# RWKV attention with a Hadamard feed-forward layer: the first two products of two tiles as one split into seven

## Chip, cores and metric

The kernel runs on one core of a Trainium2 chip. The metric is the time of one execution in device microseconds (us); it was measured three times.

## What is computed

All arrays are fp32. x is 4 x 2048 x 512, and xn is x normalized over its last axis (layer norm without weights). The result is x plus an attention part and a feed-forward part, both of xn:

```python
shifted = jnp.pad(xn, ((0, 0), (1, 0), (0, 0)))[:, :-1]
xr, xk, xv = (mu * xn + (1.0 - mu) * shifted for mu in (mu_r, mu_k, mu_v))
r, k, v = xr @ Wr.T, xk @ Wk.T, xv @ Wv.T            # 512 x 512 weights
# the recurrence over t, by batch and channel, with w_eff = -exp(w)
p   = maximum(pp, u + k_t);    e1  = exp(pp - p);           e2  = exp(u + k_t - p)
y_t = (e1 * aa + e2 * v_t) / (e1 * bb + e2)
p2  = maximum(w_eff + pp, k_t); e1b = exp(w_eff + pp - p2);  e2b = exp(k_t - p2)
aa, bb, pp = e1b * aa + e2b * v_t, e1b * bb + e2b, p2
attention = (sigmoid(r) * y) @ Wo.T
hidden = silu(xn @ W1.T) * (xn @ W3.T)               # W1, W3: 2048 x 512
feed_forward = fwht(hidden) @ W2.T                   # Walsh-Hadamard, 1/sqrt(2048)
```

## The kernel before

**Blocks and stages.** Channels lie on the partitions, tokens along the free axis. The 8192 tokens are worked on in 8 blocks of 1024 (`TB`), two blocks for a batch. A block has three stages: r, k and v (six chunks of weights), the gate and the linear part (16 tiles `j`, of 128 hidden channels each), and the down stage, which multiplies by W2 and Wo; the Hadamard transform is folded into W2 in block 0. Block 0 also makes sums of the weights on GpSimd and keeps them in DRAM (`part_w`), from which later blocks load.

**Seven products.** Matrix products are done in Strassen's manner in Winograd's form: a 2 x 2 split of weights and rows needs seven products where the plain way needs eight. A chunk of weights, loaded into a ring of three buffers (`ring_a`, by `load_parts`), holds seven forms: form 0 is the block 11 itself, form 4 the first of the sums, and so on. Channels (512) and tokens (1024) are halved; for a tile of the gate and linear part, gate (W1) and linear (W3) rows are the two halves of the weights. Each product then has 256 channels, two matmuls of 128, on 512 columns (`H`). `seven` takes five of the eight PSUM banks in turn, runs the products in the order of forms 0, 4, 5, 1, 3, 6, 2, and lets partial results move from bank to bank: ScalarE copies `pa` to `pb` after form 0, `pf` to the SBUF tile `s5` after form 4, `pb` to `pc` after form 5 and `pb` to `pd` after form 3; VectorE adds `s5` to `pb` and `pc`. `up` finishes a tile: silu(gate) * linear by tanh on ScalarE and products on VectorE, the last four of them (`tail`) in the middle of the next tile.

**The recurrence.** `wkv(h)` is written for one head of 128 channels as a generator that stops nine times. Its scans run on VectorE over 1024 tokens. A call of `step()` runs the next piece; `up` calls it twice a tile, after `h0` and after the sum on `pc`, and nine pieces of the first head are run beside r, k and v by `hook` in blocks 1 to 7. The exponents are differences from a running maximum that VectorE subtracts: `b1`, `e1b`, `e1` and `k` are each made by an instruction of their own and then go through Exp on ScalarE.

**Order.** Every engine keeps the order in which the source issues its instructions (`InOrder`, line 35 in the profile, is the line of all of them). An instruction waits on semaphores where it needs another engine's result or space, and whatever stands behind it on its engine waits with it. SyncE issues the DMAs, in the same manner.

**The down stage** already uses a second level: `Deep` splits a product on 11 once more into seven of 256 columns (`lo`, `hi`), with the banks `a`, `b` and `f`, and `s5` for `f`'s copy. `pieces_w` holds its weights, eight pieces in turn.

Of the kernel before, what the change touches and what calls it, by code (L numbers as in the profile page):

```python
# [2 lines left out]

# [37 lines left out]
def tile_rwkv_attn_hadamard_ffn(  # L41
# [36 lines left out]

    down_w = dram.tile([2, 7, KH, P, QR, P], F32, name="down_w")
    deep_w = dram.tile([6, 7, P, QR, P], F32, name="deep_w")  # L80
    stat_d = dram.tile([n_blocks, 2, TB], F32, name="stat_d")


# [6 lines left out]
    sa, sb = (const.tile([P, OFF + TB], F32, name=n) for n in ("sa", "sb"))  # L90
    e1b, e1 = (const.tile([P, TB], F32, name=n) for n in ("e1b", "e1"))
    banks = [ps.tile([P, H], F32, name=f"bank{b}") for b in range(8)]
    turn = [0]

    NP = NF // 2

# [16 lines left out]
        return flat[:, 0:size].rearrange(f"p ({' '.join(names)}) -> p {' '.join(names)}", **dict(zip(names, shape)))  # L113

    def bank():
        turn[0] += 1
        return banks[(turn[0] - 1) % 8]


    k_flat, v_flat = (t.rearrange("p b t -> p (b t)") for t in (k_sb, v_sb))  # L120
    tf_flat = tf.rearrange("p f k t -> p (f k t)")
    x_first, x_tok = (flat.rearrange("p (t c) -> p t c", c=C) for flat in (k_flat, tf_flat))
    spread = v_sb[:, 0:2, :]
    stage = [v_sb[:, 2 + s // 2, ts(s % 2, H)] for s in range(4)]
    u2_of = [e1b[:, ts(g, H)] for g in range(KH)]
# [142 lines left out]
    def wkv(h):  # L268
        w_h, u_h = weff[:, h : h + 1], vec[:, 4, h : h + 1]
        r, k, v = (row_of(kind, h) for kind in range(3))  # L270
        a0, a1, b0, b1 = sa[:, OFF - 1 : OFF - 1 + TB], sa[:, OFF : OFF + TB], sb[:, OFF - 1 : OFF - 1 + TB], sb[:, OFF : OFF + TB]
        first_a, first_b, last_a, last_b = a0[:, 0:1], b0[:, 0:1], a1[:, TB - 1 : TB], b1[:, TB - 1 : TB]
        tt, stt, scan, copy = dve.tensor_tensor, dve.scalar_tensor_tensor, dve.tensor_tensor_scan, dve.tensor_copy
        cy = [carry[:, h, n : n + 1] for n in range(3)]

        def exp(t):
            act.activation(t, t, AF.Exp)


        copy(first_a, cy[0])  # L280
        scan(a1, w_h.to_broadcast([P, TB]), k, first_a, ALU.add, ALU.max)
        tt(b1, k, a1, ALU.subtract)
        yield
        stt(e1b, a0, w_h, a1, ALU.add, ALU.subtract)
        stt(e1, k, u_h, a0, ALU.add, ALU.max)
        stt(k, k, u_h, e1, ALU.add, ALU.subtract)
        tt(e1, a0, e1, ALU.subtract)
        copy(cy[0], last_a)
        yield
        exp(b1)  # L290
        exp(e1b)
        yield

        copy(first_a, cy[1])
        tt(a1, b1, v, ALU.mult)
        scan(a1, e1b, a1, first_a, ALU.mult, ALU.add)
        copy(cy[1], last_a)
        yield
        exp(k)
        exp(e1)  # L300
        yield
        copy(first_b, cy[2])
        scan(b1, e1b, b1, first_b, ALU.mult, ALU.add)
        copy(cy[2], last_b)
        tt(v, k, v, ALU.mult)
        yield
        num, den = e1, e1b
        tt(den, e1, b0, ALU.mult)
        tt(den, den, k, ALU.add)
        dve.reciprocal(den[:, 0:H], den[:, 0:H])  # L310
        yield
        dve.reciprocal(den[:, H:TB], den[:, H:TB])
        yield
        tt(num, e1, a0, ALU.mult)
        tt(num, num, v, ALU.add)
        stt(r, r, 1.0, num, ALU.add, ALU.mult)
        stt(r, r, 0.5, den, ALU.mult, ALU.mult)
        yield
# [72 lines left out]
    def forms_in(t):  # L391
        seven_forms([t[:, n] for n in range(3, 7)], *(t[:, n] for n in range(4)))

    def load_parts(i, n):
        t = ring_a.tile([P, 7, KH, P], F32, tag="a", name=f"part_{i}_{n}")
        if is_first(i, n):
            sp.dma_start(out=t[:, 0:4], in_=wpart[n])
            forms_in(t)
        else:
            sp.dma_start(out=t, in_=part_w[n])  # L400
        return t

    def is_first(i, n):
        return i == (1 if n < 3 * KH else 0)
# [35 lines left out]
    def up(i, j, w, tail, step):  # L440

        keep_parts(i, 3 * KH + j, w)
        h0, h1 = unit(j)[:, 0:H], unit(j)[:, H:TB]

        def on11(pa):
            act.activation(h0, pa, AF.Tanh, scale=0.5)

        def on22(pa, pb, s5):
            dve.scalar_tensor_tensor(h0, h0, 1.0, pa, ALU.add, ALU.mult)
            step()  # L450
            dve.tensor_tensor(pb, pb, s5, ALU.add)

        def on12(pc, s5):
            dve.tensor_tensor(pc, pc, s5, ALU.add)
            step()

        pb, pc, pd = seven(f"{i}_{j}", w, right_of["up"], tail, on11, on22, on12)
        return (
            lambda: act.activation(h1, pc, AF.Tanh, scale=0.5),
            lambda: dve.tensor_tensor(h0, h0, pd, ALU.mult),  # L460
            lambda: dve.scalar_tensor_tensor(h1, h1, 1.0, pc, ALU.add, ALU.mult),
            lambda: dve.tensor_tensor(h1, h1, pb, ALU.mult),
        )

# [93 lines left out]
        program += deep(m, *which)  # L560
    DEEP_AT = (0, 4, 5, 6, 1, 3, 2)

    def piece(i, u):

        return pieces_w[:, (u + 4 - len(program if i else whole_program)) % 8]

    def load_piece(i, u):
        pieces = program if i else whole_program
        if u < len(pieces):
            kind, form, n = pieces[u]  # L570
            src = down_w[n[0], form, n[1]] if kind == "plain" else deep_w[form, DEEP_AT[n]]
            sp.dma_start(out=piece(i, u), in_=src)

    whole, lo, hi = slice(0, H), slice(0, H // 2), slice(H // 2, H)
    x11, x12, x22 = stage[0:2], stage[2:4], x22_of
# [19 lines left out]
    class Down:  # L595
# [21 lines left out]
            self.matmuls(pt, self.u - 1, rows, cols, start)  # L617

        def matmuls(self, pt, u, rows, cols, start=False):
            w = piece(self.i, u)  # L620
            for n in range(QR):
                pe.matmul(
                    pt[:, cols], lhsT=w[:, n, :], rhs=rows[:, n, :], start=start and n == 0, stop=n == QR - 1,
                    skip_group_check=True,
                )
# [299 lines left out]
    diag_1 = first_diagonals(1, first_statistics(1))  # L925

    def order_of(i):
        rkv, (first, *rest) = range(3 * KH), range(3 * KH, 3 * KH + NF)
        return [first, *rest] if i == 0 else [first, *rkv, *rest]

    class Chores:

# [26 lines left out]
    for i in range(n_blocks):  # L959
# [8 lines left out]
        def step():  # L968
            next(pieces, None)

        def group(n):

            order = order_of(i)
            if n + 2 < len(order):
                parts.append(load_parts(i, order[n + 2]))
            return parts.pop(0)


# [1 line left out]
        if i == 0:  # L980
            for kind, after in ((1, 2), (2, 0), (0, None)):
# [8 lines left out]
                for n in range(2 * NB):  # L990
# [11 lines left out]
                    if kind == 2 and n == 2:  # L1002
                        fold_evict(fold_products(5, NP))
                        folded = fold_butterflies()
            parts = [load_parts(i, n) for n in order_of(i)[:2]]
        else:


# [10 lines left out]
            for b in range(NB):  # L1019
                mix_here(1, b)  # L1020
            k_forms = mix_forms(1)
            tail = up(i, 0, group(0), tail, lambda: next(k_forms))
            for _ in k_forms:
                pass
            chores, hooks = mix_chores(2, 0), [0]
            for n in range(3 * KH):

                def hook():
                    hooks[0] += 1
                    for _ in range(1 if hooks[0] % 3 else 2):  # L1030
                        next(chores, None)
                    if hooks[0] in (5, 6, 8, 11, 12, 13, 14, 15, 17):
                        step()

                tail = projected_pair(i, n, group(1 + n), tail, hook)


        for j in range(0 if i == 0 else 1, NF):
            w = group(j if i == 0 else 3 * KH + j)
            if i == 0 and j <= NR:  # L1040
                if j > 1:
                    keep_down()
# [20 lines left out]
        def next_parts():  # L1063
            if not last:
                parts.extend(load_parts(i + 1, n) for n in order_of(i + 1)[:2])

        if not last:
            load_tokens(i + 1)
# [57 lines left out]
```

## Time and profile before

| | us |
|---|---|
| median of three runs | 3047.5 (3046.84 to 3048.74) |
| the profiled execution | 3048.46 |
| its span, first to last instruction | 3046.7 |
| TensorE busy | 3027.2 (99%) |
| VectorE busy | 2468.0 (81%) |
| ScalarE busy | 1014.6 (33%) |
| GpSimd busy | 231.9 (8%) |

In the profile PE is TensorE's matmuls, PEld its weight loads, DVE VectorE, ACT ScalarE, POOL GpSimd and SP SyncE. A row of a group gives line, engine, operation, output<-inputs, shape and count, then the busy time in us, the mean of one in ns, and the idle time of the engine just before them with what ended it. One matmul shows as two MATMUL records and two LDWEIGHTS. A row of the timeline gives start and duration in us, then the operation and how many follow each other. A matmul's modelled end lies beyond the start of the next, so the time that one costs is read from start to start. The cost of an instruction on VectorE and ScalarE is read likewise where the next did not wait.

### The profile page before, as it was taken

The page shows a single profiled execution, that of the slowest core. Times are in us where ns is not written, and L with a number is a line of the kernel's source. Part 1 is how long each engine was busy: PE and PEld are TensorE (multiplying, and loading weights), DVE is VectorE, ACT ScalarE, POOL GpSimd, SP SyncE. Part 2 cuts the span into 40 slices and gives each one's busy share as a digit, 9 for nine tenths or more (in the row PEclk, how much of TensorE's full clock was granted, in tenths as well). Part 3 has the DMA queues.
Part 4 walks back from the last instruction along what each step waited for, and adds up shares of the span by engine and source line. Part 5 has one row for each costly group of instructions (what it writes and reads, how often), then busy time and mean ns, then how long its engine had stood idle before and what let it go on. Part 6 is the DMA issues. An engine that isn't in the chain of part 4 may idle for free.

```text
span 3046.7 us, 24404 instructions
## 1 busy us (share of the span) xinstructions
PE 3027.2 (99%) x8492; PEld 1613.7 (53%) x8492; DVE 2468.0 (81%) x2579; ACT 1014.6 (33%) x1822; POOL 231.9 (8%) x192
## 2 busy tenths in 40 slices
PE   8999999999999999999999999999999999999999
PEld 3444444447644476444854448544484445844458
DVE  6798658897888888888887978789798887988876
ACT  4233224333243323433233332433324333243321
POOL 3363003220000000000000000000000000000000
PEclk9999999999999999999999999999999999999999
DMA  4264524666422264222632236322453224522234
GB/s 174 74 204 170 189 82 136 215 215 216 137 75 82 79 233 132 73 77 101 224 120 80 73 133 201 110 80 78 161 166 117 73 81 165 184 93 78 73 123 143
DMA packets 136058, 397.64 MB, mean 131 GB/s; under 512 B 14336, under 2 KB 32768, under 8 KB 133760
## 3 DMA queue, kind: packets, MB, share of 16 engines
q1 hardware_dynamic: 135936, 396.09, 37.8%
q8 instruction: 68, 1.11, 0.1%
q14 instruction: 54, 0.44, 0.0%
HBM read 336.08 MB, written 59.96 MB: 130 GB/s over the span
## 4 chain that ended last, share of the span: by engine, by line
PE 95%; DVE 3%; DMA 1%; POOL 1%; ACT 0%; issue 0%; SPq 0%; POOLq 0%; ACTq 0%; DVEq 0%
PE bank L35 95%; DMA pieces_w<-deep_w 1%; DVE right L35 1%; DVE e1b L35 1%; POOL rs L35 1%; DVE e L35 0%; DVE xnT L35 0%; DMA stat_d<-rs 0%; DVE sb L35 0%; DVE sa L35 0%; DVE bank L35 0%; DVE v_sb L35 0%; DMA right<-w 0%; SPq L35 0%; ACT tf L35 0%
## 5 line engine op out<-in xcount | busy, mean ns | idle before, releaser
L35 PE MATMUL bank<-tf,part 128*128 128x512 f32 x2048 | 941.7, 592 | 0.0
L35 ACT COPY bank<-bank 128x512 f32<-128x512 f32 (+1 forms) x638 | 337.1, 528 | 1414.2 <-PE bank L35 1383.7
L35 PE MATMUL bank<-right,pieces_w 128*128 128x256 f32 (+1 forms) x2928 | 791.5, 430 | 3.1 <-DVE v_sb L35 2.5
L35 PE MATMUL bank<-xnT,part 128*128 128x512 f32 x1536 | 722.1, 592 | 1.1 <-DVE right L35 1.1
L35 PEld LDWEIGHTS bank<-right,pieces_w 128*128 128x128 f32 x2928 | 557.0, 190 | 230.9 <-issue 166.9
L35 PEld LDWEIGHTS bank<-tf,part 128*128 128x128 f32 x2048 | 389.0, 190 | 490.1 <-issue 461.8
L35 PEld LDWEIGHTS bank<-xnT,part 128*128 128x128 f32 x1536 | 291.6, 190 | 366.9 <-issue 358.2
L35 DVE TENSOR_TENSOR right<-right 128x1280 f32<-128x1280 f32 (+2 forms) x236 | 327.8, 1415 | 64.7 <-PE bank L35 63.7
L35 PE MATMUL bank<-right,part 128*128 128x512 f32 x840 | 369.6, 593 | 0.0
L35 DVE SCALAR_TENSOR_TENSOR right<-right,bank 128x512 f32<-128x512 f32 x256 | 174.4, 681 | 220.5 <-ACT right L35 220.3
L35 PEld LDWEIGHTS bank<-right,part 128*128 128x128 f32 x840 | 158.4, 190 | 203.2 <-issue 189.4
L35 ACT ACTIVATE right<-bank 128x512 f32<-128x512 f32 x308 | 183.8, 600 | 124.1 <-PE bank L35 105.7
L35 DVE RECIPROCAL e1b<-e1b 128x512 f32<-128x512 f32 x64 | 214.1, 3347 | 1.1
L35 DVE TENSOR_TENSOR bank<-bank,s 128x512 f32<-128x512 f32 x256 | 168.7, 690 | 37.4 <-ACT bank L35 23.8
L35 DVE TENSOR_TENSOR right<-right,bank 128x512 f32<-128x512 f32 x256 | 173.5, 678 | 11.5 <-PE bank L35 7.1
L35 POOL TENSOR_SCALAR mean<-sums 128x8 f32<-128x8 f32 x7 | 5.8, 835 | 1870.3 <-ACT tf L35 1518.6
L35 DVE SCALAR_TENSOR_TENSOR right<-xnT,vec,right 128x1024 f32<-128x1024 f32 x92 | 119.6, 1336 | 14.3 <-ACT right L35 14.3
L35 ACT COPY s<-bank 128x512 f32<-128x512 f32 x128 | 75.0, 586 | 144.9 <-PE bank L35 144.8
L35 POOL TENSOR_TENSOR part<-part 128x256 f32<-128x256 f32 x88 | 89.4, 1027 | 200.9 <-DMA part<-wpart 99.3
L35 ACT ACTIVATE right<-xnT,omm 128x1024 f32<-128x1024 f32 x92 | 100.3, 1143 | 12.3 <-PE bank L35 12.3
L35 PE MATMUL bank<-pieces_w,part 128*128 128x512 f32 x224 | 100.7, 592 | 0.0
L35 PE MATMUL bank<-k_sb,pieces_w 128*128 128x256 f32 x420 | 97.5, 379 | 0.0
(120 smaller groups left out, 2297.9 us busy)
## 6 DMA issues: line engine op xcount, KB each, us to landing
part<-part_w SPq DMA_DIRECT2D x148, 896.0 KB, 4.6
pieces_w<-deep_w SPq DMA_DIRECT2D x294, 320.0 KB, 3.2
pieces_w<-down_w SPq DMA_DIRECT2D x80, 320.0 KB, 5.4
part_w<-part SPq DMA_DIRECT2D x22, 896.0 KB, 6.0
tf<-x SPq DMA_DIRECT2D x7, 2048.0 KB, 7.8
xnT<-xT SPq DMA_DIRECT2D x7, 2048.0 KB, 10.0
deep_w<-pieces_w SPq DMA_DIRECT2D x6, 2240.0 KB, 10.3
v_sb<-xT SPq DMA_DIRECT2D x48, 256.0 KB, 8.0
```

The lines of the kernel that those rows point to most:

```text
L35: return self.tc.keep_in_program_order(issue(*args, **kwargs))
```

## The change

From block 2 on the tiles 2 to 15 are worked on in seven pairs. For a pair, the products of form 0 (on 11) and of form 4 (the first sum) of both tiles are taken together, as one product with 256 rows of weights and 256 channels, and each of the two is split into seven products of one matmul on 256 columns. That makes 14 matmuls of 256 columns where there were 8 of 512. The five other products of each tile stay (`up_rest`).

- `make_pair` and `keep_pair` make the 14 forms of a pair in block 0 on GpSimd and write them to DRAM (`pair_w`); a pair's forms are one load of the ring, and a tile's five other forms (`rest`) another one, in two DMAs.
- `make_pair_sums` makes four sums of 256 columns for each of the two right sides, once a block, on VectorE, in `pieces_w`.
- `Pair.step` runs the seven products with numbers n = 0 to 6, in halves `lo` and `hi` of two banks, with copies on ScalarE between the halves, and sums on VectorE (`evict`).
- `up_pairs` weaves the 14 products of a pair between the products of the tile before it.
- Banks are taken from a list of free ones and given back (`take`, `give`).
- In the recurrence one difference stands for two exponents: `e1b` and `e1` are made by one instruction each, and Relu with scale 1 or -1 on ScalarE, then Exp with scale -1, makes the two from it. Three VectorE instructions of 1024 go for each head of each block, and four on ScalarE come.
- The place of a piece of `pieces_w` no longer depends on the program's length (`piece`).

```diff
         def exp(t):
-            act.activation(t, t, AF.Exp)
+            act.activation(t, t, AF.Exp, scale=-1.0)
+        def over(out, d, sign):
+            act.activation(out, d, AF.Relu, scale=sign)
         copy(first_a, cy[0])
         scan(a1, w_h.to_broadcast([P, TB]), k, first_a, ALU.add, ALU.max)
-        tt(b1, k, a1, ALU.subtract)
-        yield
-        stt(e1b, a0, w_h, a1, ALU.add, ALU.subtract)
-        stt(e1, k, u_h, a0, ALU.add, ALU.max)
-        stt(k, k, u_h, e1, ALU.add, ALU.subtract)
-        tt(e1, a0, e1, ALU.subtract)
+        stt(e1b, a0, w_h, k, ALU.add, ALU.subtract)
+        yield
+        stt(e1, k, u_h, a0, ALU.add, ALU.subtract)
         copy(cy[0], last_a)
+        over(b1, e1b, 1.0)
+        over(e1b, e1b, -1.0)
         yield
         exp(b1)
         exp(e1b)
...
         copy(cy[1], last_a)
+        over(k, e1, -1.0)
+        over(e1, e1, 1.0)
         yield
         exp(k)
         exp(e1)
...
+    def up_rest(which, tail, step):
+        j, lhs, pa, pb, s5 = which
...
+        yield
+        product(pb, 5, f2)
+        pc = take()
+        act.copy(pc, pb)
+        for f in tail:
+            f()
+        yield
+        product(pa, 1, m21)
+        act.activation(h0, pa, AF.Tanh, scale=0.5)
+        yield
+        product(pb, 3, f3)
+        dve.scalar_tensor_tensor(h0, h0, 1.0, pa, ALU.add, ALU.mult)
+        give(pa)
+        pd = take()
+        act.copy(pd, pb)
+        step()
+        dve.tensor_tensor(pb, pb, s5(), ALU.add)
+        yield
+        product(pc, 6, m22)
+        dve.tensor_tensor(pc, pc, s5(), ALU.add)
+        step()
+        yield
+        product(pd, 2, f4)
+        yield
+        return (
+            lambda: act.activation(h1, pc, AF.Tanh, scale=0.5),
+            lambda: dve.tensor_tensor(h0, h0, pd, ALU.mult),
+            lambda: dve.scalar_tensor_tensor(h1, h1, 1.0, pc, ALU.add, ALU.mult),
+            lambda: dve.tensor_tensor(h1, h1, pb, ALU.mult),
+            lambda: give(pd, pc, pb),
+        )
...
+        def step(self, d, *which):
+            q11, _, q21, q22 = pair_quarters(d)
+            t1, t2, t3, t4 = (pair_sums[:, d, n] for n in range(4))
+            for n in which:
+                if n == 1:
+                    self.banks[d] = [take(), take()]
+                a, b = self.banks[d]
+                pt, right = (
+                    (a[:, lo], q11), (a[:, hi], t1), (b[:, hi], t2), (a[:, hi], q22), (a[:, lo], q21), (b[:, hi], t3), (b[:, lo], t4),
+                )[n]
+                form = 7 * d + DEEP_AT[n]
+                pe.matmul(pt, lhsT=self.w[:, form], rhs=right, start=n == 1, stop=True, skip_group_check=True)
+                if n == 0:
+                    act.copy(b[:, hi], a[:, lo])
+                elif n == 1:
+                    act.copy(pair_s5[:, d], a[:, hi])
+                elif n == 2:
+                    act.copy(a[:, hi], b[:, hi])
+                elif n == 3:
+                    self.evict(d, 0, hi)
+                elif n == 4:
+                    self.evict(d, 0, lo)
+                elif n == 5:
+                    act.copy(b[:, lo], b[:, hi])
+                    self.evict(d, 1, hi)
+                elif n == 6:
+                    self.evict(d, 1, lo)
+
+        def evict(self, d, row, cols):
+            pt = self.banks[d][row]
+            if d and row == len(self.s5):
+                j = 2 * self.p + row
+                self.s5.append(small.tile([P, H], F32, tag="s5", name=f"s5_{self.i}_{j}"))
+            if cols == hi:
+                dve.tensor_tensor((self.s5[row] if d else pt)[:, hi], pt[:, hi], pair_s5[:, d], ALU.add)
+            elif d:
+                act.copy(self.s5[row][:, lo], pt[:, lo])
+            if d and (row, cols) == (1, lo):
+                give(*self.banks[1])
+
+        def tile(self, i, row, w):
+            at = {1: 0, 2: 1, 3: 2, 5: 3, 6: 4}
+            pa, pb = self.banks[0][row], take()
+            act.copy(pb, pa)
+            return 2 * self.p + row, lambda form: w()[:, at[form]], pa, pb, lambda: self.s5[row]
...
+                woven = (
+                    [deep(0, 1, 0)],
+                    [deep(0, 2)],
+                    [deep(0, 4, 3), deep(1, 1, 0)],
+                    [deep(0, 5), first_tile, deep(1, 2)],
+                    [deep(0, 6), deep(1, 4, 3, 5)],
+                    [deep(1, 6)],
+                )
+                tail = run(which, *woven)
+                got["w0"] = group(("rest", 3 * KH + 2 * p))
...
+                tail = run(got["first"], [], [], [], [], [second_tile])
+                got["w1"] = group(("rest", 3 * KH + 2 * p + 1))
+                which = got["second"]
...
+        if i >= 2:
+            make_pair_sums()
+            tail = up_pairs(i, group, tail, step)
+        for j in range(i, NF) if i < 2 else ():
+            if i == 0 and j % 2 and j > 1:
+                keep_pair(j // 2)
+            if i == 0 and j % 2 == 0 and j > 0:
+                make_pair(j // 2, *parts)
```

`woven` has one entry for each stop of the generator `up_rest`: what an entry names is issued after that product of the tile before. So the order on TensorE, for the first tile after which a pair begins, is: group 0's n = 1, 0; form 5; n = 2; form 1; n = 4, 3; group 1's n = 1, 0; form 3; group 0's n = 5; group 1's n = 2; form 6; group 0's n = 6; group 1's n = 4, 3, 5; form 2; group 1's n = 6. Then come the five products of the pair's first tile without anything between them.

## The prediction

> **What bounds the kernel now.** I read the page first, then busy time by stretch, then the groups by line with shapes kept apart, then the timeline.
>
> ```profile
> span 3046.7 us, 24404 instructions
> PE 3027.2 (99%) x8492; PEld 1613.7 (53%) x8492; DVE 2468.0 (81%) x2579; ACT 1014.6 (33%) x1822; POOL 231.9 (8%) x192
> PE   8999999999999999999999999999999999999999
> PEclk9999999999999999999999999999999999999999
> PE 95%; DVE 3%; DMA 1%; POOL 1%; ACT 0%; issue 0%; SPq 0%; POOLq 0%; ACTq 0%; DVEq 0%
> ```
>
> TensorE works from the first slice to the last at full granted clock, and is 95% of the chain. Busy matmuls overlap, so the question is whether records follow each other without a hole. One block's gate and linear part, by stretch:
>
> ```profile
> core 0: us, PE busy (x) PEld busy (x) DVE busy (x) ACT busy (x) POOL busy (x), PEclk, DMA share, GB/s
> 1215.00:1395.00 180.00, 180.00 (x420) 79.53 (x419) 154.15 (x163) 70.47 (x112) 0.00 (x0) 1.00 0.22 76
> ```
>
> 180 us for 420 records are 0.429 us each, one behind the other. VectorE is busy 86% of that stretch, ScalarE 39%. The next rows give the durations that I use:
>
> ```profile
> L35 PE MATMUL bank<-tf,part 128*128 128x512 f32 x2048 | 941.7, 592 | 0.0
> L35 PE MATMUL bank<-right,pieces_w 128*128 128x256 f32 x2240 | 498.0, 380 | 3.1 <-DVE v_sb L35 2.5 <-DMA pieces_w<-deep_w 0.3
> L35 ACT COPY s_d<-bank 128x256 f32<-128x256 f32 x42 | 15.7, 373 | 120.0 <-PE bank L35 120.0
> L35 DVE RECIPROCAL e1b<-e1b 128x512 f32<-128x512 f32 x64 | 214.1, 3347 | 1.1
> L35 ACT ACTIVATE sb<-sb 128x1024 f32<-128x1024 f32 x32 | 33.8, 1056 | 1.1 <-DVE sb L35 1.1
> ```
>
> ```profile
> 1102.56 2.32 PE L35 MATMUL bank<-v_sb,pieces_w 128*128 128x256 f32 x10
> 1104.72 1.46 PE L35 MATMUL bank<-right,pieces_w 128*128 128x256 f32 x6
> 1385.64 1.88 PE L35 MATMUL bank<-xnT,part 128*128 128x512 f32 x4
> 1387.36 1.88 PE L35 MATMUL bank<-tf,part 128*128 128x512 f32 x4
> ```
>
> One matmul is two records. A product of two matmuls on 512 columns takes 1387.36 - 1385.64 = 1.72 us; ten records of 256 columns take 2.16, so one matmul of 256 columns 0.432.
>
> **Saved on TensorE.** For two tiles, the products of forms 0 and 4 were 8 matmuls of 512 columns (8 x 0.858 = 6.87 us); they become 14 of 256 (14 x 0.432 = 6.04). That is 0.83 us for a pair, and 7 pairs in 6 blocks: **-34.7 us**. The five other products are unchanged: 10 of them, 17.17 us for a pair.
>
> **Waits on one bank.** Now what stands between those 14. From here 0 and 1 are the two groups of seven (on 11, on the first sum), and n is the number in `Pair.step`. The order of the built program, with what each instruction waits for, shows that n=0 waits for ScalarE's copy of n=1's half out of the same bank, in both groups, and n=3 of group 1 for the copy of n=4's half into s5. The halves differ, but the waits go by bank. Nothing else for TensorE stands in between. The price of such a round trip is in these rows:
>
> ```profile
> 588.69 0.58 ACT L35 COPY bank<-bank 128x512 f32<-128x512 f32 x1
> 589.32 0.30 PEld L35 LDWEIGHTS bank<-tf,part 128*128 128x128 f32 x2 [0.77 <-ACT bank L35]
> 589.85 0.19 PEld L35 LDWEIGHTS bank<-tf,part 128*128 128x128 f32 x1 [0.24 <-issue]
> 1213.89 3.60 PE L35 MATMUL bank<-pieces_w,part 128*128 128x512 f32 x8
> 1213.99 1.23 DVE L35 TENSOR_TENSOR sb<-k_sb,sa 128x1024 f32<-128x1024 f32 x1
> 1214.15 0.57 ACT L35 COPY bank<-bank 128x512 f32<-128x512 f32 x1 [4.63 <-PE bank L35]
> 1215.81 0.59 ACT L35 COPY s_r<-bank 128x512 f32<-128x512 f32 x1 [1.09 <-PE bank L35]
> ```
>
> A product's last record gives way at 1215.61 (1213.89 + 4 x 0.429) and its copy starts at 1215.81: 0.20. The copy of 256 columns to SBUF takes 0.37. TensorE goes on 0.05 after a copy's end (589.27 to 589.32), and its second record then comes after 0.53, where 0.43 is usual: 0.10. Together 0.73 us, three times a pair: 2.19 x 42 = **+92 us**. This alone eats the gain more than twice.
>
> The down stage has 2240 such records and 3.1 us of waits for all of them; there the product that is copied to s_d has a bank of its own. The Trainium skill, "PSUM — Partial Sum Buffer", section "PSUM bank collisions raise a hardware error", says that two engines on one bank collide whatever columns they touch, and that guards go by bank and not by address. Were they by address, the copies would run beside the next products and this term would be nothing; by bank it is the 92 us; no run here shows yet which holds.
>
> **Waits behind the recurrence.** Three more products wait for VectorE, whose instructions keep the order of the source: n=6 of group 0 for the sum on n=5's half, which stands behind one piece of the recurrence; n=6 of group 1 for a sum behind the next piece; n=1 of group 1 for a bank that the tile before gives back after `h0 * pd`. The banks now come from a list of free ones, and what is free then is what the tile before has just given back, where before they were taken in turn, five of eight for a tile. By start-to-start times, a sum of 512 columns is 0.60, of 256 0.34 to 0.42, one of 1024 that needs the one before 1.28, a scan 2.39, half a reciprocal 3.27. The nine pieces of a head cost VectorE 3.7, 1.3, 0, 3.8, 0, 3.8, 5.8, 3.3 and 4.9 us; the change has taken 3 sums of 1024 out of the second, and adds 4 sums of 256 a pair.
>
> Pair 3, counted from its first product, for all to see. The tile before has its `pa` at -5.15 (three products), and VectorE, after two tail sums, starts `h0` at -4.24 and the seventh piece at -3.64: two sums to -1.08, reciprocal to 2.2, two sums to 3.4, the eighth piece to 6.7, `h0 * pd` to 7.33. Group 1's n=1 was due at 6.32 (0.43 + 0.73 + 0.43 + 1.72 + 0.43 + 1.72 + 0.86): with 0.15 for the restart it waits 1.17. VectorE then clears three sums and `h0` by 9.5, and the ninth piece by 14.5, `pb + s5` by 15.1 and the sum by 15.5; n=6 was due at 13.39 (7.49 + 0.43 + 0.73 + 0.43 + 1.72 + 0.86 + 1.72) and waits 2.29. The next piece (3.7) makes group 1's n=6 wait 0.82. That is 4.28 us on top of 2.19.
>
> ScalarE has its own queue: four exps and relus at 0.96 to 0.98 stand in the even tiles that get two such pieces, ahead of the copy of `pa` and of n=1's. Pair 2: `pb`'s copy is through at -2.75, the four at 1.1 to 1.2, the tile's copy at 1.7, n=1's copy at 2.0; n=0, due at 0.43, waits 1.78 and not 0.73. Relu's time is not in the trace; between the 0.49 of a tanh of half the size and the 1.06 of the exp of the same size I take the exp.
>
> In the same way all seven pairs give 1.7, 2.9, 4.3, 3.1, 4.3, 4.1 and 2.6, sum 23.0 a block: 6 x 23.0 = **+138 us**. If the pieces always came late enough to be hidden it would be 0; twice as much if one late piece delays the next pair too. The same arithmetic on a block of before finds no wait, as the rows have it.
>
> **Relu elsewhere.** Blocks 1 to 7 run the first head beside r, k and v. The second piece now puts two relus on ScalarE ahead of the next chunk's first copy (the one at 1214.15), and they need a sum that ends where `sb<-k_sb,sa` ended, at 1215.2. Two relus to 1217.2, the copy to 1217.8; TensorE wants that bank at 1215.61: 2.3 us with the restart. **+16 us** in 7 blocks, 0 if the scan ran ahead. Two more such waits in blocks 0 and 1: +2.
>
> **Nothing for the rest.** VectorE loses 32 x 3 sums of 1024; it sets no end outside the pairs. In block 0 the pair forms are 56 small POOL instructions, at most 56 x 0.73 = 41 us if all were exposed; POOL is busy 118 of 320 us there. Loads: 384 KB more a pair. A pair's 896 KB and a tile's 640 KB must land within the five products of the even tile, 8.6 us; 896 KB take 4.6 from issue to landing, so at worst 9.2 one after the other, 0.6 x 36 = 22 us; I take 0, since transfers overlap.
>
> **Sum.** -34.7 + 92 + 138 + 16 + 2 = +213 us. The profiled execution took 3048.46, 1.8 more than its span, and the median is 1 below it: 3047.5 + 213 = **3260 us**.
>
> **The rivals.** (1) The halves run side by side and the pieces fit, as at the down stage with its 3.1 us: 3047.5 - 34.7 = 3013. Against it stand the waits in the built program. Chance 0.02. (2) The bank waits come, but the recurrence hides: 3047.5 - 34.7 + 92 = 3105, with relus beside r, k and v 3121. For it, VectorE is busy 86% and no more; against it, 5.8 us in one piece between sums that TensorE awaits. 0.10. (3) Lateness adds up over pairs, because VectorE has some 20 us of work in the 23.2 of a pair: 3260 + 138 = 3398. Against it, each wait of TensorE lets VectorE catch up. 0.06. (4) Loads come late as well: 3282; 0.06. Mine: 0.76, with 30% on the 138 for its own range, 3220 to 3300. Reaching to (2) and (3), the range is 3165 to 3320. A measurement of this kernel can tell about 0.2%, some 6 us, from no change. Faster 0.02 (rival 1), same 0.01, slower 0.97.
>
> **What would show it.** For each step: the 256-column records of the pairs 0.216 apart within a matmul, with three holes of 0.73 a pair that ScalarE ends, holes of 1 to 2 us that VectorE ends ahead of n=6 and of group 1's n=1, the odd pairs' in VectorE and the even ones' in ScalarE; 2.3 us at each block's third chunk; stretches of down unchanged. I am wrong if TensorE's records stay back to back across the pairs, or if the holes belong to DMA.

## The result, and the profile after

The changed kernel takes 3281.91 us (median of four runs, 3280.05 to 3288.49); the kernel before took 3048.12 beside it. The ratio is 1.0771, 95% interval 1.0752 to 1.0789: slower by 234 us, where 213 were forecast. 3281.9 lies inside the range of 3165 to 3320.

The page of the changed kernel:

```profile
span 3278.5 us, 26240 instructions
PE 3061.4 (93%) x8996; PEld 1694.9 (52%) x8996; DVE 2435.5 (74%) x2699; ACT 1227.2 (37%) x2286; POOL 259.4 (8%) x248
PE   8999999999988999889998899988999889998899
PEclk9999999999999999999999999999999999999999
PE 73%; DVE 16%; ACT 8%; DMA 1%; issue 1%; POOL 0%; SPq 0%; POOLq 0%; ACTq 0%; DVEq 0%
L36 PE MATMUL bank<-pieces_w,part_pair 128*128 128x256 f32 x672 | 202.1, 393 | 71.9 <-DVE bank L36 38.9
```

Behind the first slice, the 8s in TensorE's row stand where the gate and linear part of blocks 2 to 7 runs. The chain of work that ended last (the page's last row of shares), 95% TensorE before, now has 16% of VectorE and 8% of ScalarE. DMA stays at 1%.

I work with one more figure: for two matmul records in a row on TensorE, the difference of their starts less what a record takes at full speed (0.429 us on 512 columns, 0.216 on 256). Summed over the profiled execution these holes were 18.5 us before and 284.0 after, 265.5 more. The 34.7 saved taken off, 230.8 is left; the spans differ by 231.8. So all of the loss is in holes. By stretch, the seven pairs of a block hold 38.4 to 38.6 us of them. Who ends them, by the view of the waits (engine and what is waited for, then us in total, times, longest; PE and PEld waiting for one releaser overlap):

```profile
PEld bank L36 <- ACT pieces_w L36: 105.5, 84, 3.4
PEld bank L36 <- DVE bank L36: 73.7, 42, 2.8
PE bank L36 <- ACT pieces_w L36: 71.8, 84, 3.0
PEld bank L36 <- ACT s L36: 47.8, 42, 1.9
PEld bank L36 <- DVE s L36: 41.7, 41, 2.6
PE bank L36 <- DVE bank L36: 38.9, 36, 1.9
```

84 is two for each of 42 pairs: n=0 behind the copy of n=1's half into `pieces_w`, in both groups. 42 waits for `s` are n=3 of group 1 behind n=4's copy; the DVE rows are the sums that n=6 needs. No row of this size names a DMA: TensorE's waits for one come to 9.5 us in all, 7.9 before.

Pair 3 of block 3, whose waits the prediction worked out, in the timeline of TensorE (start, duration, then the idle time before the row):

```profile
1372.98 0.70 PE L36 MATMUL bank<-xnT,part_pair 128*128 128x256 f32 x2 [0.46 <-ACT pieces_w L36]
...
1379.25 0.70 PE L36 MATMUL bank<-pieces_w,part_pair 128*128 128x256 f32 x2 [0.84 <-DVE right L36]
1380.41 0.70 PE L36 MATMUL bank<-tf,part_pair 128*128 128x256 f32 x2 [0.46 <-ACT pieces_w L36]
...
1387.35 0.70 PE L36 MATMUL bank<-pieces_w,part_pair 128*128 128x256 f32 x2 [1.94 <-DVE bank L36]
...
1388.94 0.70 PE L36 MATMUL bank<-tf,part_pair 128*128 128x256 f32 x2 [0.46 <-ACT s L36]
...
1392.37 0.70 PE L36 MATMUL bank<-pieces_w,part_pair 128*128 128x256 f32 x2 [0.59 <-DVE s L36]
```

The view counts a record's modelled end as busy, so it shows less idle time than the hole holds. By starts, and with the 0.10 by which the second record is late, the six holes are 0.73, 1.11, 0.73, 2.21, 0.73 and 0.85 us; worked out were 0.73, 1.17, 0.73, 2.29, 0.73 and 0.82. The seven pairs of block 3 hold 4.04, 5.17, 6.36, 5.34, 6.36, 6.46 and 4.66 us; worked out, with the 2.19 of the bank trips, were 3.9, 5.1, 6.5, 5.3, 6.5, 6.3 and 4.8.

The third chunk of r, k and v in block 3, in the timeline:

```profile
1265.37 1.06 ACT L36 ACTIVATE sb<-e1b 128x1024 f32<-128x1024 f32 x1 [5.73 <-DVE e1b L36]
1266.45 1.06 ACT L36 ACTIVATE e1b<-e1b 128x1024 f32<-128x1024 f32 x1
1267.42 0.58 ACT L36 COPY bank<-bank 128x512 f32<-128x512 f32 x1
1267.93 0.58 ACT L36 COPY s_r<-bank 128x512 f32<-128x512 f32 x1
1268.05 1.98 PE L36 MATMUL bank<-pieces_w,part_full 128*128 128x512 f32 x4 [2.15 <-ACT bank L36]
```

The two relus stand ahead of the copy, each as long as an exp of the same size (1.06), and TensorE waits 2.31 + 0.10 us. That was forecast. What was not forecast comes behind such a hole, here in block 4, where the chunk's matmul starts at 1676.15 (the windows: from:to, us, PE busy, PEld, DVE, ACT, POOL, then the granted clock):

```profile
1672.00:1676.96 4.96, 2.81 (x7) 1.06 (x6) 4.92 (x6) 3.11 (x4) 0.00 (x0) 1.00 0.40 163
1676.96:1680.37 3.41, 3.41 (x5) 1.35 (x4) 0.60 (x2) 1.07 (x2) 0.00 (x0) 0.50 0.00 0
1680.37:1685.00 4.63, 4.63 (x12) 1.92 (x11) 1.51 (x2) 3.42 (x5) 0.00 (x0) 1.00 0.00 0
```

For 3.41 us the granted clock is 0.50 and the window has 5 records where some 8 fit: 1.7 us lost, by matmuls that wait for nothing. The page's clock line, a mean over 82 us for each digit, shows none of it.

The holes of the profiled executions, sorted in this way (us; "half clock" is the excess of records that took twice their time), which the experiments below are read by:

| kernel | median | blocks 0, 1 | blocks 2 to 7 | half clock | all |
|---|---|---|---|---|---|
| before | 3048.1 | 8.8 | 5.5 | 4.2 | 18.5 |
| changed | 3281.9 | 18.6 | 251.2 | 14.2 | 284.0 |
| e1_bank_order | 3296.8 | 19.5 | 229.4 | 51.5 | 300.3 |
| e2_old_recurrence | 3250.1 | 8.2 | 217.5 | 33.9 | 259.6 |
| e3_relu_alone | 3080.4 | 18.0 | 25.8 | 6.8 | 50.6 |
| e4_no_pieces | 3145.4 | 18.2 | 124.9 | 7.8 | 150.9 |
| e5_order_no_pieces | 3053.4 | 18.8 | 26.9 | 11.4 | 57.1 |
| e6_relu_in_pairs | 3263.9 | 7.9 | 235.3 | 22.4 | 265.7 |
| e7_fine_pieces | 3105.7 | 8.0 | 87.6 | 14.6 | 110.2 |
| e8_sums_early | 3137.6 | 7.5 | 120.0 | 14.4 | 141.9 |
| e9_covered_sums | 3053.6 | 11.0 | 39.9 | 7.6 | 58.6 |
| e10_fine_alone | 3108.0 | 9.2 | 96.1 | 5.9 | 111.2 |
| e11_fifteen_pieces | 3032.7 | 8.1 | 22.1 | 6.1 | 36.3 |

### The profile page after: what moved, and what is told of

Read it like the earlier page. It is cut to its first block, busy times and chain, and to the rows that moved or that the text cites. A ratio compares the mean times of both kernels' runs of the same rounds, so it can differ in the third digit from the quotient of the medians.

```text
span 3278.5 us, 26240 instructions
## 1 busy us (share of the span) xinstructions
PE 3061.4 (93%) x8996; PEld 1694.9 (52%) x8996; DVE 2435.5 (74%) x2699; ACT 1227.2 (37%) x2286; POOL 259.4 (8%) x248
## 4 chain that ended last, share of the span: by engine, by line
PE 73%; DVE 16%; ACT 8%; DMA 1%; issue 1%; POOL 0%; SPq 0%; POOLq 0%; ACTq 0%; DVEq 0%
PE bank L36 73%; DVE e1b L36 6%; DVE right L36 4%; ACT bank L36 2%; DVE bank L36 2%; DVE sa L36 2%; ACT sb L36 1%; ACT e1b L36 1%; DVE sb L36 1%; DVE e L36 1%; ACT k_sb L36 1%; DMA pieces_w<-deep_w 1%; ACT e L36 1%; ACT right L36 1%; DVE v_sb L36 1%
## 5 line engine op out<-in xcount | busy, mean ns | idle before, releaser
L36 PE MATMUL bank<-tf,part_rest 128*128 128x512 f32 x1008 | 474.0, 594 | 0.0
L36 PE MATMUL bank<-right,part_full 128*128 128x512 f32 x840 | 373.1, 598 | 0.0
L36 PE MATMUL bank<-tf,part_full 128*128 128x512 f32 x704 | 327.2, 595 | 6.4 <-ACT bank L36 6.4
L36 PE MATMUL bank<-xnT,part_rest 128*128 128x512 f32 x672 | 315.8, 592 | 0.0
L36 PEld LDWEIGHTS bank<-tf,part_rest 128*128 128x128 f32 x1008 | 192.1, 191 | 177.8 <-issue 169.4
L36 PE MATMUL bank<-pieces_w,part_pair 128*128 128x256 f32 x672 | 202.1, 393 | 71.9 <-DVE bank L36 38.9
L36 PEld LDWEIGHTS bank<-right,part_full 128*128 128x128 f32 x840 | 160.7, 193 | 208.0 <-issue 192.1
L36 PE MATMUL bank<-xnT,part_full 128*128 128x512 f32 x528 | 249.2, 594 | 1.0 <-DVE right L36 1.0
L36 PEld LDWEIGHTS bank<-tf,part_full 128*128 128x128 f32 x704 | 134.0, 191 | 168.7 <-issue 154.9
L36 DVE TENSOR_TENSOR right<-right,bank 128x512 f32<-128x512 f32 x256 | 174.1, 680 | 33.9 <-PE bank L36 29.1
L36 PEld LDWEIGHTS bank<-xnT,part_rest 128*128 128x128 f32 x672 | 127.7, 190 | 130.0 <-issue 124.8
```

Source lines behind the costliest of these rows:

```text
L36: return self.tc.keep_in_program_order(issue(*args, **kwargs))
```

## The experiments

**The order of a pair's products (e1_bank_order).** A product of 256 columns no longer follows the copy out of its own bank; another product stands between them.

```diff
                 elif n == 3:
+                    self.evict(d, 0, lo)
                     self.evict(d, 0, hi)
-                elif n == 4:
-                    self.evict(d, 0, lo)
...
-                    [deep(0, 1, 0)],
-                    [deep(0, 2)],
-                    [deep(0, 4, 3), deep(1, 1, 0)],
-                    [deep(0, 5), first_tile, deep(1, 2)],
+                    [deep(0, 1)],
+                    [deep(0, 0), deep(1, 1)],
+                    [deep(0, 2), deep(1, 0)],
+                    [deep(0, 4, 3, 5), first_tile, deep(1, 2)],
```

> The changed kernel with the order of the pair's products alone changed: n=0 of each group stands one product of the tile later than n=1, and n=4's copy into s5 is issued after n=3, so that no product of a pair follows at once the copy out of its own bank. My theory: the three holes of 0.73 us a pair go (92 us), but group 1's n=1 is now due after form 5, some 3.7 us earlier, and waits for h0 * pd there (about 5 us in pairs 3 and 5, 1 in pair 7), and form 5 of the next tile waits 1.5 to 2.5 us for its own copy in the even pairs: by the same arithmetic 34.0 us of waits a block where there were 38.4, so 3282 - 26 = 3256 us (3240 to 3270). The waits share VectorE's and ScalarE's lateness and are no sum. Rival 1, the waits add up as the prediction's sum wrote them: 3282 - 92 = 3190. Rival 2, the holes come with any 256-column matmul whose rows come from another buffer, not from the bank: 3282, holes of 0.73 still there.

Measured: 3296.80 (3294.74 to 3297.41), ratio 1.0811 (1.0795 to 1.0827). Slower than the changed kernel, where 26 us faster was expected. The waits did what the sum said: the holes of 0.73 are gone, a block's pairs hold 33.9 to 34.9 us (34.0 worked out), and blocks 2 to 7 lost 22 us of waits (251.2 to 229.4). But the remaining waits are in fewer and longer holes, and the half clock rose from 14.2 to 51.5. The longest hole in pair 3 of block 3, on TensorE and VectorE, and the granted clock around it:

```profile
1374.92 3.34 DVE L36 RECIPROCAL e1b<-e1b 128x512 f32<-128x512 f32 x1
1378.18 0.63 DVE L36 TENSOR_TENSOR right<-right,bank 128x512 f32<-128x512 f32 x1
1378.86 1.22 PE L36 MATMUL bank<-pieces_w,part_pair 128*128 128x256 f32 x2 [4.58 <-DVE right L36]
1379.88 3.62 PE L36 MATMUL bank<-xnT,part_rest 128*128 128x512 f32 x4
```

```profile
1376.94:1383.77 6.83, 4.91 (x8) 2.57 (x9) 3.15 (x4) 0.61 (x2) 0.00 (x0) 0.50 0.00 0
```

Group 1's n=1 now comes earlier, and so it waits longer for the bank that `h0 * pd` gives back behind half a reciprocal. TensorE then runs 6.83 us at half speed: four records of 512 columns take 3.62 us where 1.88 is usual. The expectation lacked the clock. Here the long waits cost more than their length.

**The recurrence without its change, and with it alone (e2_old_recurrence, e3_relu_alone).** e2 is the changed kernel with `wkv` of before; e3 is the kernel before with the new `wkv`. The diff of e3 (of e2 the reverse):

```diff
...
-        tt(b1, k, a1, ALU.subtract)
+        stt(e1b, a0, w_h, k, ALU.add, ALU.subtract)
...
-        stt(e1b, a0, w_h, a1, ALU.add, ALU.subtract)
-        stt(e1, k, u_h, a0, ALU.add, ALU.max)
-        stt(k, k, u_h, e1, ALU.add, ALU.subtract)
-        tt(e1, a0, e1, ALU.subtract)
+        stt(e1, k, u_h, a0, ALU.add, ALU.subtract)
...
+        over(b1, e1b, 1.0)
+        over(e1b, e1b, -1.0)
...
+        over(k, e1, -1.0)
+        over(e1, e1, 1.0)
```

> The changed kernel with the recurrence of before (no relu, three sums of 1024 more on VectorE for each head). My theory: the third chunk's hole goes (2.4 us in 7 blocks), block 1's extra holes (some 9 us) and the half-speed stretches behind them (some 9), and in the pairs ScalarE's queue is shorter by what VectorE's is longer: 35.3 us of waits a block by the same arithmetic, for 38.4. 3282 - 17 - 9 - 9 - 19 = 3228 us (3215 to 3245). Rival: VectorE is what holds TensorE up in the pairs, and 122 us more on it lengthen the waits: 3282 or more.

> The kernel before with the changed recurrence alone (relu on ScalarE, three sums of 1024 less on VectorE), without pairs. My theory: one hole of 2.3 us and 0.1 at the third chunk of r, k and v in each of blocks 1 to 7, 17 us, the half-speed stretches of TensorE that follow such a hole in the changed kernel's trace (1.7 us in some blocks), and waits in block 1's tiles: 3048 + 22 = 3070 us (3063 to 3080). Rival: ScalarE is idle for 60% of the time, the relus cost nothing and VectorE's relief nothing either: 3048.

Measured: e2 3250.08 (3246.05 to 3256.25), ratio 1.0654 (1.0637 to 1.0672); e3 3080.42 (3079.48 to 3081.61), ratio 1.0102 (1.0087 to 1.0118). So the relus alone make the kernel before 31 us slower, and taking them out of the changed kernel brings 32. In e3 the third chunk's hole of 2.31 + 0.10 stands in each of blocks 1 to 7 (16.9 us); in all, blocks 0 and 1 hold 9.2 us more than before, the others 20.3, and the half clock 2.6. That is 10 us more than expected of e3, and just outside its range. In e2 blocks 0 and 1 fall back to 8.2 us, and the pairs hold 35.3 us a block, as worked out; half clock, 33.9 us of it where some 5 were reckoned with, accounts for the 22 us above its expectation. The sums that the change takes from VectorE bring TensorE nothing that shows in e3; the relus that replace them stand in ScalarE's queue ahead of copies that TensorE waits for.

**The relus in the pairs only (e6_relu_in_pairs).** The changed kernel with the old recurrence in blocks 0 and 1 and for the first head.

```diff
-        pieces = (None for h in range(NB) for _ in wkv(h))
+        pieces = (None for h in range(NB) for _ in (wkv_relu if i >= 2 and h else wkv)(h))
```

> The changed kernel with the recurrence of before in blocks 0 and 1 and for the first head of every block; relu stays in heads 1 to 3 of blocks 2 to 7, so the pairs are as they were. My theory: what e3_relu_alone cost over before, 31 us, is what comes off: 3282 - 31 = 3251 us (3243 to 3260), no hole at the third chunk, 38 us of waits in each block's pairs as before. Rival: the third chunk's hole only moves, since the older recurrence there leaves VectorE later at the first pair: 3275 and more.

Measured: 3263.90 (3261.26 to 3274.28), ratio 1.0710 (1.0690 to 1.0730). The waits fell as forecast, by 10.7 us in blocks 0 and 1 and by 15.9 in the others (the third chunks), 26.6 together; the time fell by 18.0 where 31 were expected, because 8.2 us of half clock came in. That the stretches of half clock moved to other places and did not go was not expected.

**The pairs without the recurrence (e4_no_pieces, e5_order_no_pieces).** Both leave out the recurrence of heads 1 to 3 in blocks 2 to 7; e5 has the order of e1 besides.

```diff
-            tail = up_pairs(i, group, tail, step)
+            tail = up_pairs(i, group, tail, lambda: None)
...
-        for _ in pieces:
+        for _ in pieces if i < 2 else ():
```

> The changed kernel without the recurrence of heads 1 to 3 in blocks 2 to 7 (left out altogether, so the attention part of those channels is wrong); pairs as they are. My theory: of the waits in a block's pairs only the three of 0.73 us a pair, and two at the first pair, stay: 16.9 us where there were 38.4, 129 us less in six blocks: 3282 - 129 = 3153 us (3138 to 3166). Rival: TensorE waits for the pair's own copies and sums, which the recurrence only happens to stand beside: over 3230.

> Both: the order of e1_bank_order and the recurrence of heads 1 to 3 left out in blocks 2 to 7, as in e4_no_pieces. My theory: no hole is left in the pairs but 0.7 us at the first of each block, so what remains is the 34.7 us saved, 17 us at the third chunk and some 20 us in block 1 and in TensorE's half-speed stretches: 3282 - 226 = 3056 us (3045 to 3066). So the order is worth 97 us here, and a quarter of that with the recurrence there. Rival, additive waits: 3153 - 92 = 3061 here and 3190 for e1_bank_order. Rival, the splitting itself costs TensorE time beyond its records: over 3090.

Measured: e4 3145.37 (3143.82 to 3147.16), ratio 1.0315 (1.0300 to 1.0331); e5 3053.43 (3051.43 to 3060.48), ratio 1.0016 (1.0006 to 1.0026). Without pieces, the pairs of e4 hold 87.9 us of holes, and 14.9 by which the second records behind them are late. Six of a block's seven pairs hold 2.19 us each, three bank trips to the hundredth; the first holds 3.8. In e5 the pairs hold 3.2. So the same new order is worth 92 us here (3145.4 to 3053.4) and costs 15 in e1. By block, the pairs hold 38.4 us with the trips and the recurrence, 34.5 with the recurrence alone (e1), 16.9 with the trips alone (e4) and 0.6 with neither (e5). So these are not two terms that can be taken away one after the other: while TensorE waits for a bank, VectorE catches up.

**Shorter pieces (e7_fine_pieces, e8_sums_early).** If long pieces hold back the sums, short ones with relus spread out should not. The recurrence of heads 1 to 3 from block 2 on is cut into 16 pieces, the old one runs elsewhere, steps are called at places worked out from the durations of the profiles, a pair's sums and copies out of a bank come after the last product on it, and the tail of a tile is issued ahead of form 5 (the lines of the last two are not printed). In both kernels group 1's n=6 stood behind the load that refills its ring place, so it multiplied with the next pair's weights, and at pair 7 with data that the down stage's load had put in its place; their times hold a wait for that load.

```diff
+FINE_ORDER = ['p1', 'p2+p3', 'r1', 'r2', 'x1', 'x2+r3', 'p7+r4', 'p8+x3', 'x4', 'p11', 'p12', 'p13', 'p14', 'p15', 'p16', 'p17']
...
+                    [deep(0, 1)],
+                    [deep(0, 0)],
+                    [deep(0, 2), deep(1, 1)],
+                    [deep(0, 4, 3, 5), first_tile, deep(1, 0)],
+                    [deep(0, 6), deep(1, 2)],
+                    [deep(1, 5, 4, 3)],
...
-                tail = run(which, *woven)
+                tail = run(which, *woven, at=(0, 1, 3, 3))
...
-                tail = run(got["first"], [], [], [], [], [second_tile])
+                tail = run(got["first"], [deep(1, 6)], [], [], [], [second_tile], at=(0, 1))
```

p are parts of VectorE (p14 and p15 half a reciprocal each), r relus, x exps; `at` names the products after which a piece runs. e8 puts the sum on n=5's half ahead of n=6 again, in both groups, and group 1's products in the order 4, 3, 5.

> A version made after the theory: relu as in e6_relu_in_pairs; the order of the pair's products such that each copy has a product of 1.7 us beside it (group 0: n=1, 0, 2 one product apart, then 4, 3, 5, then 6; group 1 one later, its n=6 ahead of the next tile); the sum on n=5's half issued after n=6; the tail of a tile issued ahead of form 5; the recurrence in 16 pieces of at most 3.3 us for a head where there were 9, four in the first tile and two in the second of a pair's span. My theory: of 38.4 us of waits in a block's pairs 2.6 are left, so 3048 - 34.7 + 6 x 2.6 = 3029 us (3020 to 3040), faster than before. Rival: the split has a cost of its own beside the waits (the loads, the sums, TensorE's clock), which e5_order_no_pieces did not show for want of the recurrence: 3048 or more.

> e7_fine_pieces with one thing put back: the sum on n=5's half is issued before n=6, as in the change (and group 1's 4, 3, 5 in that order, as its tiles ask). My theory: n=6 of group 1 waits for VectorE again, 1.2 to 1.9 us a pair, 10.2 us a block for 2.6: 3029 + 46 = 3075 us (3060 to 3090). Rival: with small pieces VectorE is on time, and where the sum stands does not matter: 3029.

Measured: e7 3105.67 (3104.01 to 3106.69), ratio 1.0185 (1.0169 to 1.0200); e8 3137.58 (3137.33 to 3139.67), ratio 1.0291 (1.0276 to 1.0307). 77 and 63 us above what was expected. In e7's view of the waits:

```profile
PE bank L37 <- DMA pieces_w<-deep_w: 51.1, 11, 9.0
```

In each of six blocks 8 to 10 us are lost at pair 7, and some 2 in the other pairs. The load's wait came with the place that I had given n=6 and not with the change; between the two kernels the early sum costs 32 us, where 46 were worked out.

**The product back in its place (e9_covered_sums, e10_fine_alone).** e9 mends e7; e10 is e9 with the changed kernel's order of the products.

```diff
-                    [deep(1, 5, 4, 3)],
+                    [deep(1, 5, 4, 3, 6)],
...
-                tail = run(got["first"], [deep(1, 6)], [], [], [], [second_tile], at=(0, 1))
+                tail = run(got["first"], [], [], [], [], [second_tile], at=(0, 1))
```

> As e7_fine_pieces (other order of the pair's products, recurrence of heads 1 to 3 from block 2 on in 16 shorter pieces with the relus, the old recurrence elsewhere), but group 1's n = 6 stands in the first tile's span again, straight behind n = 5, 4 and 3, before the ring place of the pair's weights is given to the next pair: it reads this pair's weights, as in the changed kernel. e7 lost 9.1 us at pair 7 to a load that this product had to wait for, and some 2 to 3 us to half clock behind that wait, six times; the waits that it had besides were 1.5 to 2 us a block. Here, laid along the order of the products with the durations of the profiles before and after, 2.6 us of waits a block are left, in four holes, none over 1.1 us. 3048 - 34.7 (fewer columns) + 6 x 2.6 = 3029; range 3022 to 3040, TensorE's clock at full in blocks 2 to 7. Rival theory (the pairs cost something that no wait shows, for instance more loads or short matmuls that run below the cadence of the long ones): not below 3048.

> As e9_covered_sums, with the changed kernel's order of the pair's products, so that each product of 256 columns again follows the copy out of the bank that it writes: two round trips of 0.73 us a pair are back (n = 0 behind n = 1's copy in both groups; the third, n = 4 behind n = 3's copy, has been taken away by the later copies and stays away), 14 in a block of seven pairs, and 0.8 us more at pair 1: 12.4 us of waits a block where e9 has 2.6. Expected 6 x 9.8 = 59 over e9: 3088 (3075 to 3100). If the pieces alone made the difference and the order were hidden by then, it would stand within 10 us of e9; if the order alone did it, it would be near the 3282 of the changed kernel.

Measured: e9 3053.62 (3051.23 to 3055.05), ratio 1.0017 (1.0008 to 1.0026); e10 3108.03 (3105.48 to 3110.40), ratio 1.0196 (1.0183 to 1.0210). The order is worth 54 us here (59 expected). A block's pairs hold 2.4 us in e9 (2.6 worked out) and 12.5 in e10 (12.4). In e10's view of the waits the two trips a pair are back, 84 times and none over 1.8 us, where the changed kernel has up to 3.4; five of a block's seven pairs hold 1.46 us, two trips at their bare price:

```profile
PEld bank L37 <- ACT pieces_w L37: 78.2, 84, 1.8
PE bank L37 <- ACT pieces_w L37: 44.5, 84, 1.4
```

Both stand 20 to 25 us above their expectations, and so the rival of e9 (not below 3048) looked right. The timeline of e9 shows where, and that it isn't the pairs:

```profile
1438.02 3.35 DVE L37 RECIPROCAL e1b<-e1b 128x512 f32<-128x512 f32 x1
...
1442.43 3.34 DVE L37 RECIPROCAL e1b<-e1b 128x512 f32<-128x512 f32 x1
...
1449.64 2.32 PE L37 MATMUL bank<-right,pieces_w 128*128 128x256 f32 x10
1450.04 1.22 DVE L37 SCALAR_TENSOR_TENSOR right<-right,e1b 128x1024 f32<-128x1024 f32 x1
1451.18 0.68 DVE L37 TENSOR_TENSOR right<-right,bank 128x512 f32<-128x512 f32 x1
...
1453.09 1.48 DVE L37 TENSOR_TENSOR right<-right 128x1280 f32<-128x1280 f32 x1
...
1453.53 0.33 ACT L37 COPY bank<-bank 128x256 f32<-128x256 f32 x1
...
1454.68 3.56 PE L37 MATMUL bank<-right,pieces_w 128*128 128x256 f32 x10 [2.71 <-ACT bank L37]
```

This is the down stage. The last pieces of the recurrence, two halves of a reciprocal among them, stand in front of the last tile's sums (the rows from 1451.18 on); the sum for the right side of the down stage (1453.09) is late with them, and TensorE waits 2.9 us, in each of blocks 2 to 7. The view names ScalarE, whose copy had ended 0.8 us before; VectorE's sum ends at 1454.57, 0.1 before TensorE goes on. My arithmetic had stopped at the last tile.

**Fifteen pieces (e11_fifteen_pieces).** One piece fewer for each head, so that three are left for the last tile and not six.

```diff
-FINE_ORDER = [..., 'p8+x3', 'x4', 'p11', 'p12', ...]
+FINE_ORDER = [..., 'p8+x3', 'x4+p11', 'p12', ...]
...
-                tail = run(which, at=(0, 1, 2, 3, 4, 5))
+                tail = run(which, at=(0, 1, 2))
```

> As e9_covered_sums, but the recurrence of a head is in 15 pieces (the fourth exponential and the second sum's scan are one piece), so that three pieces and not six are left for the last tile of the feed-forward layer. e9 stood at 3053.6, 24 over what was expected, and its trace shows where: in each of blocks 2 to 7 TensorE waits 2.6 to 2.9 us at the tenth product of the down layer or so, since VectorE still had the last pieces of the recurrence in front of the last tile's products, and half of these holes are followed by 1.3 to 1.5 us of half clock; 6 x 2.8 + 4.2 = 21. Here the same arithmetic, carried on into the down layer (for e9 it gives 3.2 us there), has no such wait, and 0.5 us more in the pairs. Expected 3053.6 - 21 + 3 = 3035 (3028 to 3043), faster than before. Rival theory (the wait in the down layer comes from its loads and not from the recurrence's last pieces): 3053 or more again.

Measured: 3032.70 (3030.53 to 3035.97) beside 3050.38 for the kernel before, ratio 0.9944 (0.9930 to 0.9957). Faster than both kernels. The waits of 2.9 us are gone in all six blocks, so they came from the recurrence's last pieces and not from the loads. Its page:

```profile
span 3030.9 us, 26415 instructions
PE 3003.9 (99%) x8996; PEld 1704.6 (56%) x8996; DVE 2474.5 (82%) x2741; ACT 1164.7 (38%) x2230; POOL 273.7 (9%) x248
PE 92%; DVE 6%; DMA 1%; POOL 0%; ACT 0%; issue 0%; SPq 0%; ACTq 0%; DVEq 0%
```

The same 8996 records on TensorE as in the changed kernel, back to 99% of the span. Its holes are 36.3 us, 17.8 more than before; with the 34.7 saved that makes 16.9, and the spans differ by 15.8. The gain is the change's own saving less these holes: blocks 2 to 7 of the kernel before had 5.5 us of holes, so shorter pieces alone could not have brought it. How much each of the other parts of e7 to e11 is worth (16 pieces or 15, their places, the tail ahead of form 5, relus in the pairs only) was not taken apart; tried singly were the order (54 us) and the place of the sum (32).

## Why the prediction was right, and where its size was off

- **Saved on TensorE, -34.7.** Confirmed: the span grew by the holes less this, to 1 us; and e11 brings it out as a gain.
- **Waits on one bank, +92.** Confirmed: three holes of 0.73 a pair, ended by ScalarE; in e4, without the recurrence, 2.19 us in six of a block's seven pairs, and 102.8 in all (87.9 + 14.9) with some 1.6 more at each first pair; gone in e5. Whether halves of one bank could run side by side was open on the trace of before. In the built order the program's waits keep them apart, as the rule of the Trainium skill, "PSUM — Partial Sum Buffer", section "PSUM bank collisions raise a hardware error", asks for. No run here let them run side by side.
- **Waits behind the recurrence, +138.** Confirmed nearly hole by hole. With the bank trips, 38.4 us a block were worked out and 38.4 to 38.6 are measured. The 138 is what the recurrence adds while the trips are there; with the trips taken away (e1) it holds 34.5 us a block by itself, which the sum does not say. Blocks 2 to 7 hold 245.7 us more than before without the half clock; 92 + 138 and six third chunks at 2.3 make 243.8.
- **Relu elsewhere, +16.** Confirmed: 2.31 + 0.10 in blocks 1 to 7.
- **"Two more such waits in blocks 0 and 1: +2."** Mis-sized. Blocks 0 and 1 hold 9.8 us more than before; with block 1's third chunk, 4.3 were forecast. Two relus stand ahead of a copy three times more, in the gate and linear part: holes of 1.82 us at 241.8 in block 0 and of 1.49 and 3.58 at 534.3 and 647.4 in block 1, together 6.9. e3 has the same three (1.26, 0.86 and 3.49), e2 and e6 have none of them.
- **Nothing for the rest.** Confirmed: POOL's pair forms and the loads end no hole of note in the changed kernel.
- **Missing from the sum: half clock, +10.0.** 14.2 us after, 4.2 before. I priced a wait by its length, and waits of 2 us and more can also slow the matmuls behind them.

The 5.5 and 10.0, with 1.9 in the pairs, are 17.4 of the 20.8 us by which the change of the median was under-forecast. Of the rest, 1 lies in the span outside the holes, and 2 in the medians: the changed kernel's lies 1.7 above its profiled execution, the other's 0.3 below.

Rival (1), halves side by side, and (2), the recurrence hides, are out by the holes. Rival (3), lateness that adds up, is out: the pairs wait as each was worked out alone. Rival (4), loads late as well, names a time (3282) that came true by chance: TensorE's waits for DMA grew by 1.6 us and not by 22. Of the eleven expectations only those of e4, e5 and e11 held the time within their range; that the order of e1 would bring 26 us (it lost 15), and that e7's pieces were all it took, fell outright. The waits in the pairs came out within 1 us a block wherever they were worked out, but for e7 and e8 with their load; what was missed lay elsewhere, in half clock, in that load and in the down stage.

## What to carry to other kernels

When a product is split into halves that share a bank, put another product between a half's copy and the next product on that bank, and then look at what the in-order engines have in front of the sums that TensorE needs next: neither alone was enough here (against the changed kernel the order cost 15 us, the shorter pieces with later sums, and the relus in the pairs only, brought 174, both 228, and 234 are needed to come back to the kernel before), and only together, with the queue cleared as far as the next stage, did the split pay. Price a wait on TensorE by more than its length if it reaches 2 us, and carry the working on until the queue that was made late has caught up.

## What the runs showed of the hardware

TensorE's granted clock falls to 0.50 for stretches of 3.41 us, or two or three times that (three times only in e7 and e8, at the waits for the load), whose starts lie on a fixed grid: in the changed kernel they begin at 857.76, 1096.70 and 1676.96, which are 70 and 170 steps of 3.413 us apart. The thirteen profiles (from 40 us to the last matmul) can be divided into the windows of that grid, and the idle time between matmul records summed in each. In all 105 full-speed windows that half clock followed, 2.08 us or more was idle; in the other 11,500 or so at most 2.17. So whether a hole of 2.3 us costs 1.7 more depends on whether it falls into one window or across two, and several short holes can do it together. The changed kernel has a hole of 2.31 to 2.36 us at the third chunk of seven blocks: half clock followed five of them, and not those at 472.58 and 1268.05. This would explain why removing waits in e2 and e6 moved the stretches of half clock, and probably part of why runs of one kernel differ; neither was tried by itself. The Trainium skill, "TensorE: Matmul & The Clock Gate", section "Part 1: The HAM clock gate (the "warmup" mystery)", describes a free-running window of 3413 ns, and the grid agrees; it puts the fall after an idle window of about 3.4 us, and here some 2.1 to 2.2 us inside a window were enough.
